# A graph layer whose lags are taken in one by one at the end, with its row fetches, register loads and feature loads regrouped

## Chip, core and metric

The kernel runs on one core of one Trainium2 chip. The time is device microseconds of one execution. Lower is better. Engines are named as in the profile: PE is TensorE (PEld its weight loads), DVE is VectorE, ACT is ScalarE, POOL is GpSimd, SP is SyncE. A queue's name with a q (SPq) means what the engine's sequencer does itself: register loads, semaphore waits, issuing of DMAs.

## The reference, cut to what matters

There are 12500 nodes with 64 features each and 200000 edges, sorted by their target node `dst`. For every edge a gate is computed from its 64 edge features and a message from the features of both end nodes; the messages are summed by target; a two-layer network on the sum is added to the node, and the result is layer-normalised.

```python
ssp = lambda x: softplus(x) - log(2)
nodes = node_state[edges].reshape(num_edges, -1)          # source and target rows, 128 wide
gates = ssp(edge_state @ We1 + be1) @ We2 + be2
gates = gates * (1 - sigmoid(5 * (edges_distance - 3.5)))
h = ssp(nodes @ Wn1 + bn1) @ Wn2 + bn2
message_sum = zeros.at[edges[:, 1]].add(h * gates)
new_state = node_state + (ssp(message_sum @ Ws1 + bs1) @ Ws2 + bs2)
out = layernorm(x + new_state)
```

## The kernel before

**Groups.** The edges are cut into 391 groups of 512, numbered g (line 62 on has the constants). As the edges are sorted by target, the 256 edges of each half of a group have targets in a window of 42 nodes, whose first node `base` is computed on the chip in a preparation stage (to about 150 us), which also builds a table of the target-side products x·Wn1+bn1.

For each group these steps exist, each a small function:

- `gather(g)` (line 166): four indirect DMAs on POOL (line 176) fetch the 512 source rows, 20 groups ahead. In a few groups, `by_rows`, only three are used: the fourth block of 128 rows comes through SP, row by row.
- `fetch(i)` (line 180): in step i SP loads ROWS = 4 row numbers into registers by one register load (line 187) and issues four one-row DMAs (line 191) into the tile `xr`. 128 rows take 32 steps, so every 32nd group is served so: 12 groups. A slot's group is transposed two steps after the step that fetches its last row.
- `load(g)` (line 195): SP fetches the group's edge features `eT` (128 KB, line 197), every second time loads four window bases into registers (line 199), and fetches two windows of 42 table rows into `wns` (line 204). It runs five groups ahead; eT and wns have seven buffers.
- `transposes` and `xcopy` (lines 217, 222): PE transposes the rows, ACT copies them out.
- `layer1_edge`, `layer1_node` (226, 228, 233): first layers into the PSUM tile `z` (two buffers).
- `exps`, `logs` (243, 246, ACT), `softplus` (251, DVE): the activation `s`.
- `layer2_edge`, `layer2_node` (257, 260, 265): second layers into `gh`.
- `hcut`, `message` (270, 274, DVE): the product of gate, cutoff and h.
- `scatter` (278, PE): one-hot matrices add the messages up by window. `window` (284, 287, DVE): each half's base goes into a register by a load of its own, then 42 columns are added to `sums`.

**Order of the work.** The order on each engine is that of the program; the scheduler is off. Step i of the main loop holds `load(i+5)`, `fetch(i)`, `gather(i+19)`, the scatter of group i-3, the second layers of group i-1, the first layers of i+1 and the transposes of i+3. So a group passes with lags of three, two and two steps. On PE a step runs: scatter, `layer2_edge`, first layers, (a node block's matmul), transposes, `layer2_node`. On DVE: softplus, window, hcut, message, one-hot. At step `both`, 12 before the last, all lags are cut at once: two groups of second layers in that step, three scatters in the next. The last group's first layer is split in two.

**Node blocks.** When all edges up to a block of 512 nodes are known to be summed (`block_steps`), the block's own network runs in five parts, one per step, between the groups: `hidden` and `clamp`; `logs` and `ssp`; `layer2` and `center`; `square` and `variance`; `root` and `store`. The block's x rows `y` are fetched by SP in `clamp` (line 312), and SP issues the store of the result in `store` (line 360), which waits for DVE's last product `y` (line 359). SP's order is that of the program, so what is behind the store waits with it. The last 512 nodes are two blocks of 256, run side by side at the end.

Of the kernel before, what the change touches and what calls it, by code (L numbers as in the profile page):

```python
# [63 lines left out]
CATCH_UP = 12  # L65
ROWS = 4
# [6 lines left out]
def node_blocks(N):  # L73

    rest = N - NB
    first = rest % NB
    assert rest > 0 and first % 2 == 0 and first <= HE
    sizes = ([first] if first else []) + [NB] * (rest // NB) + [HE, HE]
    return [(sum(sizes[:i]), n) for i, n in enumerate(sizes)]
# [12 lines left out]
def slots_by_rows(NG):  # L92

    return [g for g in range(P // ROWS + 4, NG - 2, P // ROWS)]
# [3 lines left out]
def gnn_resnorm_kernel(ctx: ExitStack, tc: tile.TileContext, a: dict, out: bass.AP, E: int):  # L98
# [52 lines left out]
    half = const.tile([P, 1], F32, name="half")  # L151
    ones3 = const.tile([PIECES, HE], BF16, name="ones3")
# [26 lines left out]

    def fetch(i):  # L180

        n, r = divmod(i * ROWS, P)
        if i < 0 or n >= len(by_rows):
            return
        if r == 0:
            xrs[by_rows[n]] = loads.tile([P, P], F32, name="xr", bufs=2)
        _, at = nc.values_load_multi_w_load_instructions(
            rows_i[n : n + 1, r : r + ROWS], engines=[SP], min_val=0, max_val=N - 1,
            skip_runtime_bounds_check_because="src holds rows of x")
        for j, v in enumerate(at):  # L190
            nc.sync.dma_start(xrs[by_rows[n]][r + j : r + j + 1, :D], x[bass.ds(v, 1), :])  # L191
# [3 lines left out]
    def load(g):  # L195
        eTs[g] = loads.tile([P, HE], F32, name="eT")
        nc.sync.dma_start(eTs[g], a["eT"][:, g, :])
        if g % 2 == 0:
            _, at = nc.values_load_multi_w_load_instructions(
                base_i[0:1, 2 * g : 2 * g + 4], engines=[SP], min_val=0, max_val=N - 1,  # L200
                skip_runtime_bounds_check_because="they were clamped to these bounds")
            bases[g], bases[g + 1] = at[:2], at[2:]
        for h in range(2):
            nc.sync.dma_start(wns[D:DW, g % REST, h, :], table[bass.ds(bases[g][h], W), :])  # L204
# [26 lines left out]
    def layer1_node(g, h):  # L231
        zn = zs[g][:, h, HE * (1 - h) : HE * (2 - h)]
        nc.tensor.matmul(zn, wns[:, g % REST, h, :], xTs[g][:, h], start=True, stop=True, skip_group_check=True)  # L233
# [29 lines left out]
    def layer2_node(g, h):  # L263
        for t in range(2):
            nc.tensor.matmul(ghs[g][:, 1, 2 * t + h, :], ss[g][:, 1 + h, t, :], wn2, start=False,  # L265
                             stop=h == 1 and t == 1, skip_group_check=True)
# [14 lines left out]

    def window(g):
        for h in range(2):
            base = nc.values_load(base_i[0:1, 2 * g + h : 2 * g + h + 1], engines=[DVE], min_val=0, max_val=N - 1,
                                  skip_runtime_bounds_check_because="it was clamped to these bounds")
            part = sums[h * D : (h + 1) * D, bass.ds(base, W)]
            nc.vector.tensor_add(part, part, scs[g][h * D : (h + 1) * D, h * W : (h + 1) * W])  # L287

    def node_block(first, n, pool):
# [20 lines left out]
        def clamp():  # L310
            t["y"] = tile3("y")
            nc.sync.dma_start(t["y"], x[rows, :].rearrange("(q p k) d -> p q k d", q=nq, k=2))
            t["l"], t["zb"] = (pool.tile([P, HE], F32, name=name, bufs=2) for name in ("l_s", "zb"))
            nc.vector.tensor_scalar(t["l"], t["z"], packed["bs1"], BIG, OP.add, OP.min)
            nc.vector.tensor_scalar(t["zb"], t["z"], packed["bs1"], None, OP.add)
# [17 lines left out]
        def center():  # L333
            nc.vector.scalar_tensor_tensor(t["y"], t["y"], 2.0, t["u"][:, :nq], OP.mult, OP.add)
            mean = small("mean")
            nc.vector.tensor_reduce(mean, t["y"], AX.X, OP.add)
            nc.vector.scalar_tensor_tensor(t["y"], mean.to_broadcast([p, nq, 2, D]), -1.0 / D, t["y"], OP.mult, OP.add)
# [5 lines left out]
        def variance():  # L343
            t["v"] = small("var")
            nc.vector.tensor_reduce(t["v"], t["y2"], AX.X, OP.add)
            nc.vector.tensor_scalar(t["v"], t["v"], 1.0 / D, EPS, OP.mult, OP.add)

        def root():
            t["r"] = small("rstd")
            nc.scalar.activation(t["r"], t["v"], AF.Ln)  # L350
            nc.scalar.activation(t["r"], t["r"], AF.Exp, scale=-0.5)

        def store():

            v, r = t["v"], t["r"]
# [4 lines left out]
            nc.sync.dma_start(out[rows, :].rearrange("(q p k) d -> p q k d", q=nq, k=2), t["y"])  # L360

        def then(f, g):
            def both():
# [4 lines left out]
        return [(hidden, clamp), (None, then(logs, ssp)), (layer2, center), (None, then(square, variance)),  # L368
                (None, then(root, store))]
# [6 lines left out]
    with tc.manual_schedule():  # L376
# [4 lines left out]
        with tc.tile_pool(name="prep", bufs=1) as prep:  # L381
# [23 lines left out]
            nc.vector.memset(half, 0.5)  # L405
            nc.vector.memset(ones3, 1.0)
# [40 lines left out]
            nc.vector.tensor_add(brow[:, 1:3, :], brow[:, 1:3, :], ps[:1, : 2 * D].rearrange("o (i d) -> o i d", d=D))  # L447
            pieces = prep.tile([1, PIECES, 4 * D], BF16, name="pieces")
# [43 lines left out]
        with tc.tile_pool(name="finish", bufs=1) as finish:  # L492
            blocks = list(zip(node_blocks(N), block_steps(N, NG)))
            last = NG - 1
            both = last - CATCH_UP
            second, third, ahead = {}, {}, {}
            for i in range(-3, NG + 1):
                groups = [i - 1] if i < both else [i - 1, i] if i == both else [i]
                second[i] = [g for g in groups if 0 <= g < NG]
                groups = [i - 3] if i <= both else [i - 3, i - 2, i - 1] if i == both + 1 else [i - 1]  # L500
                third[i] = [g for g in groups if g >= 0]
                groups = [i + 3] if i < both else [] if i == both else [i + 2]
                ahead[i] = [g for g in groups if g < NG]
            todo, complete = [], 0
# [9 lines left out]
            for i in range(-3, NG + 1):  # L514
                part = todo.pop(0) if todo else None
# [4 lines left out]
                if i < both:  # L520
                    if 0 <= i + 1:
                        zs[i + 1] = z_tile()
                    for g in third[i]:
                        scatter(g, zs[i + 1][:, 1, HE : HE + 2 * W])
                    for g in second[i]:
                        layer2_edge(g)
                elif i + 1 < last:
                    zs[i + 1] = z_tile()
                if i + 1 < last:
                    at(layer1_edge, i + 1)  # L530
                    at(layer1_node, i + 1, 0)
                    at(layer1_node, i + 1, 1)
                if part and part[0] and i + 2 < last:
                    part[0](tx_tile())
                for g in ahead[i]:
                    transposes(g)
                if i + 1 < last:
                    at(exps, i + 1)
                    if i < both:
                        at(logs, i + 1)  # L540
                for g in ahead[i]:
                    xcopy(g)
                if i >= both and i + 1 < last:
                    logs(i + 1)
                if i + 2 == last:
                    zs[last] = z_tile()
                    layer1_edge(last)
                for g in second[i]:
                    if i >= both:
                        layer2_edge(g)  # L550
                    if i + 2 == last:
                        layer1_node(last, 0)
                        layer1_node(last, 1)
                    layer2_node(g, 0)
                    layer2_node(g, 1)
                if i + 2 == last:
                    for some in (edge, node):
                        exps(last, some)
                        logs(last, some)
                if i + 1 < last:  # L560
                    at(softplus, i + 1)
                if i >= both:
                    for g in third[i][:-1]:
                        scatter(g, tx_tile()[:, : 2 * W])
                        window(g)
                    for g in third[i][-1:]:
                        scatter(g, tx_tile()[:, : 2 * W])
# [3 lines left out]
                for g in third[i][-1:]:  # L571
                    window(g)
                    complete = g + 1
                if i < both:
                    for g in second[i]:
                        hcut(g)
                        message(g)
                for g in ahead[i]:
                    at(onehot, g + 2)
                if i + 2 == last:  # L580
                    softplus(last, edge)
                    softplus(last, node)
                if part:
                    if i + 2 < last:
                        part[1]()
                    else:
                        node_part(part)
                while blocks and blocks[0][1] <= complete and i < last:
                    todo += node_block(*blocks.pop(0)[0], finish)
# [151 lines left out]
```

## Time and profile before

| | |
|---|---|
| median of 14 runs | 2598.84 us (2572.59 to 2615.81) |
| the profiled execution | 2610.76 us |
| its span, first to last instruction | 2609.0 us |
| mean granted TensorE clock | 0.828 |
| PE busy | 2237.2 us (86%) |
| POOL busy | 1468.6 us (56%), 1551 gathers of 947 ns |
| DVE, ACT busy | 1046.6 us (40%), 918.0 us (35%) |
| rows fetched by SP | 1536 DMAs of 0.2 KB |
| eT and wns | 391 DMAs of 128 KB, 782 of 21 KB |

The page counts register loads, moves, semaphore waits and the issuing of DMAs as no engine's busy time, so SP has no row in its first part; what SP does is seen in the timeline of SP, in the waits of the SP queue, and in the view of one source line. A PE that is busy for 86% need not be PE at its peak: the granted clock enters the durations.

### The profile page before, as it was taken

How to read it: one execution, taken by the hardware profiler on the slowest of the kernel's cores; microseconds unless marked ns; L12 is line 12 of the kernel's file. 1: busy time of each engine (PE TensorE's matmuls, PEld its weight loads, DVE VectorE, ACT ScalarE, POOL GpSimd, SP SyncE). 2: the span in 40 equal slices, each digit the busy share in tenths (PEclk: the TensorE clock that was granted, in tenths of full speed). 3: DMA queues.
4: the chain of work that ended last, by engine and by line, in shares of the span. 5: the costliest groups of instructions: out<-in, count | busy, mean ns of one | idle time of the engine just before them, and what ended most of it. 6: DMA issues, size and time to landing. Idle time of an engine off the chain costs nothing.

```text
span 2609.0 us, 42101 instructions
## 1 busy us (share of the span) xinstructions
PE 2237.2 (86%) x11378; PEld 1776.7 (68%) x11378; DVE 1046.6 (40%) x2752; ACT 918.0 (35%) x1322; POOL 1468.6 (56%) x1555
## 2 busy tenths in 40 slices
PE   4469888899888979898988978988999987998997
PEld 4357677677676757676777767766777765776775
DVE  4123333333444333333434443443444443444455
ACT  1133333333333323333333333333333333333443
POOL 6655666556666546655556656565566655565500
PEclk9977888677888778878879788787788877888887
DMA  7212222222222222222222222222222222222210
GB/s 196 79 46 51 50 51 53 48 49 54 50 49 52 49 50 51 54 50 52 49 53 53 51 53 48 53 51 53 53 56 51 51 50 54 55 54 55 54 47 18
DMA packets 171021, 143.15 MB, mean 55 GB/s; under 512 B 46507, under 2 KB 142947, under 8 KB 170778
## 3 DMA queue, kind: packets, MB, share of 16 engines
q1 hardware_dynamic: 119778, 87.95, 11.7%
q0 software_dynamic: 49632, 50.92, 10.8%
q10 hardware_dynamic: 1368, 1.51, 0.3%
q8 instruction: 95, 1.56, 0.3%
q14 instruction: 148, 1.21, 0.2%
HBM read 130.57 MB, written 9.63 MB: 54 GB/s over the span
## 4 chain that ended last, share of the span: by engine, by line
PE 77%; issue 9%; another core or an unknown queue 3%; DVE 3%; SPq 3%; ACT 2%; DMA 1%; POOL 1%; DVEq 0%; ACTq 0%; POOLq 0%
PE z L233 15%; PE gh L265 13%; PE z L228 10%; PE gh L260 10%; PE z L278 8%; PE tx L217 8%; PE gh L257 5%; PE z L226 3%; SPq L191 1%; PE tx L306 1%; PE z L471 1%; PE tx L330 1%; DVE h L270 1%; SPq L204 1%
## 5 line engine op out<-in xcount | busy, mean ns | idle before, releaser
L176 POOL DMA_INDIRECT xg<-in_x,src_i x1551 | 1468.4, 947 | 1002.3 <-issue 376.4
L251 DVE SCALAR_TENSOR_TENSOR s<-u,z 128x768 f32<-128x768 f32 x392 | 372.8, 951 | 1249.5 <-ACT u L246 708.8
L243 ACT ACTIVATE u<-z 128x768 f32<-128x768 f32 x392 | 317.0, 809 | 1491.2 <-PE z L233 537.1
L233 PE MATMUL z<-xT,wns 106*128 106x256 f32 x1564 | 516.6, 456 | 43.1 <-issue 37.6
L265 PE MATMUL gh<-consts,s 128*128 128x64 f32 x3128 | 456.5, 296 | 8.1 <-issue 8.1
L265 PEld LDWEIGHTS gh<-consts,s 128*128 128x128 f32 x3128 | 452.4, 222 | 4.7 <-issue 4.7
L233 PEld LDWEIGHTS z<-xT,wns 106*128 106x128 f32 x1564 | 358.5, 231 | 134.4 <-issue 64.9
L246 ACT ACTIVATE u<-u,one 128x768 f32<-128x768 f32 x392 | 365.9, 933 | 12.4
L278 PE MATMUL z<-xg,msg 128*128 128x84 f32 x1500 | 268.1, 306 | 108.0 <-DVE msg L274 43.9
L260 PE MATMUL gh<-consts,s 128*128 128x128 f32 x1564 | 326.8, 336 | 27.8 <-issue 18.9
L228 PE MATMUL z<-eT,consts 128*128 128x256 f32 x782 | 327.8, 504 | 19.8 <-issue 13.2
L260 PEld LDWEIGHTS gh<-consts,s 128*128 128x128 f32 x1564 | 240.7, 218 | 140.9 <-issue 129.6
L278 PEld LDWEIGHTS z<-xg,msg 128*128 128x128 f32 x1500 | 224.7, 215 | 121.9 <-issue 80.4
L217 PE MATMUL tx<-consts,xg 128*106 128x128 f32 x1552 | 286.8, 316 | 6.8 <-DVE xg L209 2.7
L217 PEld LDWEIGHTS tx<-consts,xg 128*106 128x106 f32 x1552 | 230.3, 156 | 72.9 <-issue 28.5
L222 ACT COPY xT<-tx 106x512 f32<-106x512 f32 x391 | 221.8, 567 | 63.4 <-PE tx L217 48.4
L270 DVE TENSOR_TENSOR h<-gh,cut 128x256 f32<-128x256 f32 x391 | 165.9, 424 | 178.0 <-PE gh L265 86.8
L228 PEld LDWEIGHTS z<-eT,consts 128*128 128x128 f32 x782 | 137.4, 218 | 79.9 <-issue 38.5
L257 PE MATMUL gh<-row,ones 3*128 3x512 bf16 x391 | 166.6, 426 | 6.6 <-issue 6.5
L274 DVE TENSOR_TENSOR msg<-gh,h 128x256 f32<-128x256 f32 x391 | 165.9, 424 | 13.5
L287 DVE TENSOR_TENSOR sums<-sums,z 64x42 f32 x750 | 144.4, 193 | 13.6 <-issue 7.2
L209 DVE TENSOR_TENSOR xg<-consts,rel 128x168 f32<-128x168 f32 x391 | 126.7, 325 | 1.1 <-issue 0.4
(79 smaller groups left out, 625.7 us busy)
## 6 DMA issues: line engine op xcount, KB each, us to landing
eT<-in_eT SPq DMA_DIRECT2D x391, 128.0 KB
xg<-in_x,src_i POOLq DMA_INDIRECT x1551
xr<-in_x SPq DMA_DIRECT2D x1536, 0.2 KB
wns<-table SPq DMA_DIRECT2D x782, 21.0 KB
table<-tb SPq DMA_DIRECT2D x14, 448.0 KB
sums<-in_xT SPq DMA_DIRECT2D x7, 455.0 KB
y<-in_x SPq DMA_DIRECT2D x23, 128.0 KB
out<-y SPq DMA_DIRECT2D x23, 128.0 KB
```

What stands on the lines that cost most here:

```text
L176: nc.gpsimd.indirect_dma_start(out=xg[:, k, :D], out_offset=None, in_=x, in_offset=bass.IndirectOffsetOnAxis(ap=src_i[:, g, k : k + 1], ax ...
L217: nc.tensor.transpose(tx[:, k, :], row, ident)
L222: nc.scalar.copy(xT, xTs[g])
L228: nc.tensor.matmul(zs[g][:, 0, :HE], we1.rearrange("a h d -> a (h d)"), eTs[g], start=False, stop=True, skip_group_check=True)
L233: nc.tensor.matmul(zn, wns[:, g % REST, h, :], xTs[g][:, h], start=True, stop=True, skip_group_check=True)
L243: nc.scalar.activation(us[g][:, part], z_of(g)[:, part], AF.Exp)
L246: nc.scalar.activation(us[g][:, part], us[g][:, part], AF.Ln, bias=one)
L251: nc.vector.scalar_tensor_tensor(ss[g].rearrange("p i t e -> p (i t e)")[:, part], us[g][:, part], BIG, z_of(g)[:, part], OP.min, OP.max)
L257: nc.tensor.matmul(gh, ones3[:, :P], row3.rearrange("q i k d -> q (i k d)"), start=True, stop=False, skip_group_check=True)
L260: nc.tensor.matmul(v[:, 0, t], ss[g][:, 0, t, :], we2, start=False, stop=False, skip_group_check=True)
L265: nc.tensor.matmul(ghs[g][:, 1, 2 * t + h, :], ss[g][:, 1 + h, t, :], wn2, start=False, stop=h == 1 and t == 1, skip_group_check=True)
L278: nc.tensor.matmul(sc, msgs[g][:, 2 * t : 2 * t + 2, :].rearrange("p h f -> p (h f)"), xgs[g][:, 2 * t : 2 * t + 2, D:DW], start=t == 0, s ...
```

## The change

Five things are changed together.

1. SP's row fetch: six rows a step instead of four, eight row numbers by one register load; slots need no longer start at a step's first row. 128 rows take 21.3 steps, which makes 17 slots instead of 12; a slot's group lies two steps later behind its last row than before.
2. SP's loads: `eT` of two groups by one DMA of 256 KB; the window bases of four groups (eight registers) by one register load.
3. DVE's `window` loads the two bases of a group by one register load.
4. Node blocks: 25 of them, the last of 512; the bias and the weights of the last layer are centred in the preparation, and x rows are fetched and centred four and two groups before the block is complete, so that after `layer2` only an addition is left; eps enters as ACT's bias; the store is a part of its own and is issued by ACT, but for the last block.
5. The order: in a step `layer2_node` now follows `layer2_edge` before the first layers. The lags are shortened one at a time, from 30 steps before the last; the last group is written out.

```diff
-CATCH_UP = 12
-ROWS = 4
+CATCH_UP = 30
+ROWS = 6
+REGS = 8
...
 def fetch(i):
-    n, r = divmod(i * ROWS, P)
...
-    _, at = nc.values_load_multi_w_load_instructions(
-        rows_i[n : n + 1, r : r + ROWS], engines=[SP], ...)
-    for j, v in enumerate(at):
-        nc.sync.dma_start(xrs[by_rows[n]][r + j : r + j + 1, :D], x[bass.ds(v, 1), :])
+    for at in range(ROWS * i, min(ROWS * (i + 1), len(by_rows) * P)):
+        n, r = divmod(at, P)
...
+        if at % REGS == 0:
+            _, row_at[:] = nc.values_load_multi_w_load_instructions(
+                rows_i[n : n + 1, r : r + REGS], engines=[SP], ...)
+        nc.sync.dma_start(xrs[by_rows[n]][r : r + 1, :D], x[bass.ds(row_at[at % REGS], 1), :])
...
 def slots_by_rows(NG):
-    return [g for g in range(P // ROWS + 4, NG - 2, P // ROWS)]
+    ends = [ceil(P * (n + 1) / ROWS) + 6 for n in range(NG)]
+    return [g for g in ends if g < NG - 2]
...
 def load(g):
-    eTs[g] = loads.tile([P, HE], F32, name="eT")
-    nc.sync.dma_start(eTs[g], a["eT"][:, g, :])
     if g % 2 == 0:
+        pair = loads.tile([P, 2, HE], F32, name="eT", bufs=LOADS // 2 + 2)
+        for j in range(min(2, NG - g)):
+            eTs[g + j] = pair[:, j, :]
+        nc.sync.dma_start(pair[:, : min(2, NG - g)], a["eT"][:, g : min(g + 2, NG), :])
+    if g % 4 == 0:
+        n = min(4, NG - g)
         _, at = nc.values_load_multi_w_load_instructions(
-            base_i[0:1, 2 * g : 2 * g + 4], engines=[SP], ...)
+            base_i[0:1, 2 * g : 2 * (g + n)], engines=[SP], ...)
...
 def window(g):
+    if g not in window_at:
+        window_bases(g)
     for h in range(2):
-        base = nc.values_load(base_i[0:1, 2 * g + h : 2 * g + h + 1], engines=[DVE], ...)
-        part = sums[h * D : (h + 1) * D, bass.ds(base, W)]
+        part = sums[h * D : (h + 1) * D, bass.ds(window_at[g][h], W)]
...
-        return [(hidden, clamp), (None, then(logs, ssp)), (layer2, center), (None, then(square, variance)),
-                (None, then(root, store))]
+        return [(None, fetch), (None, center), (hidden, clamp), (None, then(logs, ssp)), (layer2, add),
+                (None, then(square, variance)), (None, then(root, scale)), (None, store)]
...
+        def store():
+            queue = nc.sync if first + n == N else nc.scalar
...
     for i in range(-3, NG):
-        groups = [i - 1] if i < both else [i - 1, i] if i == both else [i]
+        groups = [i - 1] if i < ends + 6 else [i - 1, i] if i == ends + 6 else [i]
...
-        groups = [i - 3] if i <= both else [i - 3, i - 2, i - 1] if i == both + 1 else [i - 1]
+        groups = ([i - 3] if i < ends - 6 else [i - 3, i - 2] if i == ends - 6 else [i - 2]
+                  if i < ends + 12 else [i - 2, i - 1] if i == ends + 12 else [i - 1])
...
-        ahead[i] = [g for g in groups if g < NG]
+        ahead[i] = [i + 3] if i < ends else [i + 2] if i == ends + 1 else [i + 1] if i > ends + 2 else []
...
+    if i < ends:
...
+        for g in second[i]:
+            layer2(g)
+        if i >= -1:
+            layer1(i + 1)
```

## Prediction

> **What bounds the kernel now.** I read the page's first two parts, then the busy time by stretches, then SP's timeline, then who waits for whom. PE is the busiest engine, but the stretches show that it is not simply full. The columns below are the stretch, its length, busy time and count of the edge matmul's two passes (two per group, so half the count is the number of steps) for PE and for PEld, then clock, DMA share and GB/s.
>
> ```profile
> 160.00:2410.00 2250.00, 298.82 (x714) 125.03 (x712) 0.82 0.22 52
> 2478.00:2510.00 32.00, 4.89 (x14) 2.08 (x14) 1.00 0.16 44
> 2510.00:2565.00 55.00, 7.68 (x16) 3.19 (x16) 0.72 0.15 40
> ```
>
> In the long stretch 357 steps take 2250 us, 6.30 us each, at clock 0.82. From 2478 us on, when POOL has issued its last gather (2470.20), seven steps take 32 us, 4.57 each, at full clock. So PE can do a step in 4.6 us and has 6.3. The clock follows: where PE waits it falls, and then PE is slow for a while. Who makes PE wait? SP's timeline, first without gathers, then with them (start, time from first issue to last, line, count):
>
> ```profile
> 2481.93 0.36 SPq L197 DMA_DIRECT2D eT<-in_eT  x1
> 2482.54 0.88 SPq L204 DMA_DIRECT2D wns<-table  x2
> 2484.25 1.50 SPq L191 DMA_DIRECT2D xr<-in_x  x4
> 2485.84 0.36 SPq L197 DMA_DIRECT2D eT<-in_eT  x1
> 2486.99 0.92 SPq L204 DMA_DIRECT2D wns<-table  x2
> 2488.73 1.50 SPq L191 DMA_DIRECT2D xr<-in_x  x4
> 2490.28 0.41 SPq L312 DMA_DIRECT2D y<-in_x  x1
> 2490.79 0.41 SPq L197 DMA_DIRECT2D eT<-in_eT  x1
> ```
>
> ```profile
> 1306.92 0.70 SPq L197 DMA_DIRECT2D eT<-in_eT  x1
> 1309.06 0.53 SPq L204 DMA_DIRECT2D wns<-table  x2
> 1310.77 1.55 SPq L191 DMA_DIRECT2D xr<-in_x  x4
> 1313.79 0.01 SPq L197 DMA_DIRECT2D eT<-in_eT  x1
> ```
>
> From eT to eT SP needs 3.91 us, and 4.44 with a base load (2485.84 to 2490.79 less 0.51 for y): 4.18 on average, with no pause worth the name. With gathers running the same round takes 6.87 here, and 6.30 on average, since SP goes round once per PE step. So about 2.1 us of a round are added while POOL gathers; the trace shows that, not its cause. Is SP waiting in them? The waits of the SP queue between 160 and 2478 us (total, times, longest):
>
> ```profile
> SPq L191 <- DMA xr<-in_x: 28.7, 54, 1.2
> SPq L360 <- DVE y L359: 24.1, 5, 6.8
> SPq L197 <- PE tx L217: 8.9, 24, 0.7
> SPq L204 <- PE tx L217: 8.7, 29, 0.7
> ```
>
> All rows of that answer sum to some 105 us of 2318, none but the store's is over 1.2 us. So **SP is at work or slowed for over 95% of the main loop and is never held back by full buffers**: whatever is added to its round has nowhere to hide. And PE does wait for it, at the transposes of the row-fetched groups (busy, mean | idle before, releasers):
>
> ```profile
> L217 PE MATMUL tx<-consts,xr 128*106 128x128 f32 x12 | 4.6, 387 | 47.8 <-DMA xr<-in_x 23.8 <-DMA wns<-table 22.5 <-issue 1.5
> L278 PE MATMUL z<-xg,msg 128*128 128x84 f32 x1500 | 268.1, 306 | 108.0 <-DVE msg L274 43.9 <-issue 34.2 <-DVE h L270 22.6
> ```
>
> Twelve instructions have 47.8 us of idle before them: PE had run ahead of SP and is pulled back. The 108.0 us before the scatters are the other loop, ACT and DVE late with a message. Both are near the limit; I take SP as the one that sets the pace.
>
> **The change by its parts, per step.**
>
> *Rows.* Four rows span 1.50 us with the last issue's 0.23 (median of L191 in its source view: 228 ns), so one row is (1.50-0.23)/3 = 0.42. Two more: **+0.84**.
>
> *Register loads.* The source views give
>
> ```profile
> L187 SPq TENSOR_LOAD <-rows_i x384: 2/552/746, 151.0 to 2541.8; - x192
> L284 DVEq TENSOR_LOAD <-base_i x782: 297/303/599, 163.1 to 2594.1; - x196
> ```
>
> 303 ns for one register, 490 (L199's median) to 552 for four. Eight are not in the trace: at least 0.55, at most two loads, 1.10. I take 490-303 over three registers, 0.06 each, and so 0.80, nearest to the measured slope. Rows: 0.75 loads a step of 0.80 for one of 0.55, **+0.05** (-0.14 to +0.28). Bases: a load costs 0.53 of a round now (4.44-3.91), every second step; then 0.78 every fourth: **-0.07**.
>
> *Feature pair.* One eT issue with what precedes it is about 0.46 (0.36 and 0.10 ahead); half of them go: **-0.23**. That a transfer of 256 KB issues in the time of one of 128 KB is assumed; at twice the time the gain is zero.
>
> *Store.* 24 issues go to ACT, 0.46 each: -0.03 on SP. On ACT they come in front of the next exponential, 24 x 0.46 = 11 us in all, while ACT is busy for 35%; in a part of its own the store follows finished work.
>
> SP's own round: +0.84+0.05-0.07-0.23-0.03 = **+0.56** on 4.18. Now cover: waits that disappear once SP is the late one are the store's 24 us and the waits for PE's releases, about 50 us together in the same answer, so 75 us or 0.21 a step. Net **+0.35 a step**. Row fetching lasts 363 steps: 0.35 x 363 = +127 us. Bounds: if the slow part of a round grows with the work (6.30/4.18), 0.56 becomes 0.84, net +0.63, +229 us; if SP has cover that I don't see, 0.
>
> *Five gathers fewer* (17 slots for 12): 5 x between 0.5 (a quarter of the 2.1 us) and 2.1 us: -3 to -10, I take -7. The gathers' POOL time (5 x 0.95) lies beside PE's.
>
> *DVE's base load.* One load of 0.30 less per step, and 0.06 longer. Both loads run while the softplus does (0.95 us, L251), which hides them; where the softplus comes late up to 0.3 x 357 = 107 us of DVE's chain could go, but with SP late it is not what ends last: 0.
>
> *`layer2_node` moved.* The eight matmuls (0.84 us at full clock in the chain) now lie before the first layers. hcut's 178 us of idle on DVE shrink, z comes 0.84 us later to ACT, and the scatter's wait for the message grows by up to that. Behind it on PE stand the whole step's matmuls. Against 0.84 x the 95 waits that the scatters of the main loop have at most (80 us) stands the same sum earlier for hcut: 0, either way hidden behind SP.
>
> *Node blocks.* The same reductions and products, two steps earlier: beside other work, 0. One block fewer: one `hidden` and one layer2, 2 us of PE.
>
> *The end.* From 2510 to 2565 us eight steps take 55 us, 6.9 each, against 4.57 just before: all lags fall at once, PE waits, the clock drops. If the gradual cut avoids half of the 8 x 2.3 us: -10 (0 to -19). The tail is one block of 512, whose operations take 0.42 where the half blocks' take 0.29, but no centring stands in it: -2 (0 to -3).
>
> Sum: 127-7-2-10-2 = **+106**. The execution's own time of 2610.8 becomes 2717; it stands 12 us above the median of the 14 runs, so against the median I say **2705 us**.
>
> **A rule against this.** Six one-row DMAs have 0.2 KB each, and SP's sequencer still spends 0.42 us on every one. The Trainium skill, "DMA: Bandwidth & Descriptors", section "Issuing engines are not separate DMA queues", holds the sequencer's time to start a DMA to be usually small beside the DMA itself; by it the two rows would cost nothing, and the sum would be near 2580. Here the issue times fill SP's round, so the row decides. The same page ("Latency and other measured facts") puts a register load's floor at about 600 ns, whatever it loads; by it eight registers cost 0.60, not 0.80, and the sum is 0.20 x 0.75 + 0.05 = 0.20 a step, 72 us, lower. The single load's 303 ns on DVE contradicts the floor.
>
> **Rivals.**
>
> 1. *SP isn't the limit* (faster). For it: TensorE is 86% busy, most idle time before PE's matmuls is put to issue and messages, not to DMAs, and a slot's rows now have two steps more before they are needed. Then the 47.8 us before xr go, the end gives 12, the gathers 7, the block 2: 2611-69 = 2542, against the median 2530; if only half of the xr idle goes, 2554. Price point: net SP work of at most 0 a step. Chance 0.28, at 2520 to 2585.
> 2. *SP's added work is covered* by fewer slow spells: PE's runs at 4.6 us a step crowd POOL's gathers together, and a slower, steadier step would space them. If the slow part falls by a sixth (2.1 to 1.75), +0.35 is gone and the end's gains remain with some wait for SP: 2590 to 2610. Chance 0.10.
> 3. *The slow part grows with SP's work*: 2609+229-21, about 2805 on the median. Chance 0.10.
> 4. The forecast, SP sets the pace with +0.2 to +0.5 a step: 2640 to 2760. Chance 0.52.
>
> The bound of 0.5% is about what a measurement of this kernel can tell from no change. Faster 0.28, same 0.10, slower 0.62. For 8 in 10 the range must take in most of rival 1 and leave out rival 3's end: 2535 to 2770. The likeliest case's own range is 2640 to 2760.
>
> **What would show it.** In the changed profile: rows issued x6 in 2.3 to 2.4 us; an eT issue every second step; SP's round near 6.6 us with gathers and near 4.7 without; idle on PE before L228 and L233 put to eT and wns, and a lower clock. The register load of eight at 0.75 to 0.85. Steps from 2510 us on without a drop of the clock. I am wrong if SP's queue shows waits for PE's releases, that is, slack, and steps stay at 6.3 or fall; or if the idle before xr is gone and nothing takes its place.

## The result, and the profile after

The changed kernel takes **2874.70 us** (median of 10 runs, 2860.07 to 2888.69), before takes 2600.44 (47 runs): ratio **1.1067** [1.1038, 1.1097]. The forecast was 2705. The profiled execution spans 2899.6 us for 2609.0, at a mean clock of 0.763 for 0.828.

The kernel before itself took about 2600 us in the recorded comparison, in e5 to e8 and (2570) in e16, and about 2000 us in all other experiments, on chips 0 and 14 both, so what follows speaks of a 2600 group and a 2000 group and compares only within one; after as it stands was run in the 2600 group alone.

The changed kernel, by stretches (edge matmuls alone; length, PE, PEld, clock, DMA share, GB/s):

```profile
160.00:2410.00 2250.00, 292.14 (x649) 121.59 (x648) 0.76 0.20 47
2740.00:2790.00 50.00, 6.98 (x14) 2.89 (x14) 0.71 0.10 28
```

Where before made 357 steps in 2250 us, after makes 324: 6.93 us a step instead of 6.30. And after the last gather (2736.8 us) seven steps now take 50 us, 7.1 each, where they took 4.57. So there are two losses, one in the loop and one in the end. SP's timeline beside the gathers, for six rows a round, and the waits of SP's queue from 160 to 2740 us:

```profile
1306.17 3.37 SPq L196 DMA_DIRECT2D xr<-in_x  x6
1309.56 0.70 SPq L205 DMA_DIRECT2D eT<-in_eT  x1
1312.45 1.46 SPq L214 DMA_DIRECT2D wns<-table  x2
1316.04 3.68 SPq L196 DMA_DIRECT2D xr<-in_x  x6
```

```profile
SPq L196 <- DMA xr<-in_x: 32.0, 68, 1.3
SPq L196 <- DMA out<-y: 23.7, 1, 23.7
SPq L214 <- PE tx L227: 17.9, 61, 0.6
SPq L205 <- PE z L238: 16.6, 11, 6.1
```

Six rows take 3.4 to 3.7 us here. Where no register load falls among the six, the median in the main loop is 3.38 us, against 2.32 in e9, which has no slow instructions. SP still waits for nobody for long, the one 23.7 us apart. Then the groups that wait:

```profile
L238 PE MATMUL z<-eT,consts 128*128 128x256 f32 x782 | 354.8, 544 | 78.6 <-DMA eT<-in_eT 77.6 <-issue 0.7
L296 PE MATMUL z<-xg,msg 128*128 128x84 f32 x1432 | 267.2, 321 | 134.6 <-DVE msg L292 113.1 <-DVE h L288 12.4 <-issue 6.2
L341 DVE TENSOR_REDUCE mean<-y 128x4 f32<-128x256 f32 x24 | 10.0, 419 | 200.1 <-DMA y<-in_x 200.1
```

The first is the wait that the forecast named (features that SP brings late). The last is one that it priced at nothing: DVE's centring stands 200 us waiting for the rows `y`, and the scatters behind it wait for DVE's message (113.1 us, 43.9 before).

The same by stretches of steps, in us, from the start of the first edge matmul of each step (group 10's, 340's and so on) in the profiled executions of the 2600 group (the two executions of the unchanged kernel, after and e5, agree to 3 us in the main loop):

| | to step 10 | 10 to 340 | 340 to 360 | 360 to 390 | tail | span |
|---|---|---|---|---|---|---|
| before | 195.6 | 2088.6 | 123.6 | 172.4 | 28.7 | 2609.0 |
| e8: before, new loads, four rows | 195.6 | 2025.8 | 124.5 | 167.7 | 29.3 | 2542.9 |
| e16: before, SP's part whole | 190.4 | 2165.4 | 128.6 | 168.4 | 28.0 | 2680.8 |
| e7: after, early y, late lag | 192.6 | 2266.8 | 139.8 | 208.0 | 27.4 | 2834.5 |
| e6: after, early y | 199.4 | 2265.6 | 171.1 | 180.1 | 27.5 | 2843.7 |
| e5: after, repeated | 194.8 | 2295.9 | 179.3 | 198.2 | 22.7 | 2890.8 |
| after | 192.7 | 2298.7 | 179.0 | 201.7 | 27.6 | 2899.6 |

### The profile page after: what moved, and what is told of

It reads as the page before. It is cut to its first block, busy times and chain, and to the rows that moved or that the text cites. A ratio compares the mean times of both kernels' runs of the same rounds, so it can differ in the third digit from the quotient of the medians.

```text
span 2899.6 us, 43084 instructions
## 1 busy us (share of the span) xinstructions
PE 2411.7 (83%) x11373; PEld 1899.9 (66%) x11373; DVE 1045.6 (36%) x2750; ACT 926.9 (32%) x1317; POOL 1465.8 (51%) x1550
## 5 line engine op out<-in xcount | busy, mean ns | idle before, releaser
L245 PE MATMUL z<-xT,wns 106*128 106x256 f32 x1564 | 571.2, 496 | 79.8 <-DMA wns<-table 59.6
L279 PE MATMUL gh<-consts,s 128*128 128x64 f32 x3128 | 501.1, 309 | 61.0 <-issue 60.3
L279 PEld LDWEIGHTS gh<-consts,s 128*128 128x128 f32 x3128 | 486.5, 234 | 68.5 <-issue 68.0
L245 PEld LDWEIGHTS z<-xT,wns 106*128 106x128 f32 x1564 | 380.6, 251 | 203.7 <-issue 63.2
L238 PE MATMUL z<-eT,consts 128*128 128x256 f32 x782 | 354.8, 544 | 78.6 <-DMA eT<-in_eT 77.6
L296 PE MATMUL z<-xg,msg 128*128 128x84 f32 x1432 | 267.2, 321 | 134.6 <-DVE msg L292 113.1
L296 PEld LDWEIGHTS z<-xg,msg 128*128 128x128 f32 x1432 | 249.8, 246 | 152.1 <-issue 119.9
L273 PE MATMUL gh<-consts,s 128*128 128x128 f32 x1564 | 335.0, 346 | 11.2 <-DVE s L264 9.3
L273 PEld LDWEIGHTS gh<-consts,s 128*128 128x128 f32 x1564 | 248.4, 227 | 124.1 <-issue 111.3
L227 PE MATMUL tx<-consts,xg 128*106 128x128 f32 x1547 | 310.3, 336 | 15.8 <-issue 10.4
L227 PEld LDWEIGHTS tx<-consts,xg 128*106 128x106 f32 x1547 | 248.0, 168 | 85.1 <-issue 44.8
L238 PEld LDWEIGHTS z<-eT,consts 128*128 128x128 f32 x782 | 147.6, 236 | 143.7 <-DMA eT<-in_eT 87.5
```

The source lines that it names most:

```text
L227: nc.tensor.transpose(tx[:, k, :], row, ident)
L238: nc.tensor.matmul(zs[g][:, 0, :HE], we1.rearrange("a h d -> a (h d)"), eTs[g], start=False, stop=True, skip_group_check=True)
L273: nc.tensor.matmul(v[:, 0, t], ss[g][:, 0, t, :], we2, start=False, stop=False, skip_group_check=True)
L296: nc.tensor.matmul(sc, msgs[g][:, 2 * t : 2 * t + 2, :].rearrange("p h f -> p (h f)"), xgs[g][:, 2 * t : 2 * t + 2, D:DW], start=t == 0, s ...
```

## The experiments

Two theories went in. **S**: SP's own round is the whole loss. **O**: the new order, the node blocks and the end make it, by new waits.

**e1 to e4: one part undone or done alone (2000 group).** Edits, cut to the lines that differ:

```diff
-ROWS = 6                                  # e1, on after
+ROWS = 4
-    return [g for g in ends if g < NG - 2]    # e4, on after: one slot only
+    return [g for g in ends if g < NG - 2][:1]
-... [i - 3] if i < ends - 6 else [i - 3, i - 2] if i == ends - 6 ...   # e3, on after
+... [i - 3] if i < ends else [i - 3, i - 2] if i == ends ...
```

e2 is before with after's `fetch`, `load`, `slots_by_rows`, ROWS and REGS, and nothing else.

> The changed kernel with four rows a step instead of six, all else as changed. Theory S (SP's round sets the pace of the main loop, and its own work is stretched by about a half while POOL gathers): SP's own round falls to some 3.7 us, stretched 5.5, so SP no longer sets the pace; steps of the main loop fall from 6.9 to 6.0-6.3 us and the time to 2580-2660 us; what stays above the kernel before is the slower end. Theory O (the new order and the new waits, above all DVE waiting for the early fetch of y, set the pace): the time stays over 2800 us.

> The kernel before with only SP's part of the change: six rows a step, registers by eight, the feature pair, bases for four groups. Theory S: 2600 + 0.6 to 0.7 us for 363 steps, 2790 to 2860 us. Theory O: 2580 to 2640 us.

> The changed kernel, but the scatter's lag is cut from three to two only when the step's order changes (at 30 before the last), not six steps earlier. If the six steps between 354 and 360, which took up to 11.7 us each, are slow because their scatter waits for a message of the step just before, the time falls by 25 to 45 us to about 2840. If they are slow because SP is behind there, it stays within 15 us of 2875.

> The changed kernel with one row-fetched group instead of 17: SP fetches rows in the first 22 steps only, and POOL makes 16 gathers more. Theory S: SP's own round is then about 1.7 us, SP is never late, and the time falls to 2560-2650 us; idle of PE before the edge and table matmuls that is put to DMAs goes to under 10 us. Theory O: over 2800 us.

Measured: e1 2049.26 us, ratio 1.0274 [1.0230, 1.0318]; e2 2005.93, 1.0060 [1.0037, 1.0083]; e3 2166.79, 1.0863 [1.0832, 1.0895]; e4 2073.83, 1.0397 [1.0367, 1.0427]. The absolute numbers expected don't apply, as before takes 1994 here. The order of the four does: SP's part alone costs 0.6%, after without it 3 to 4%, both together 8.6%. ("Both together" is e3, after but for the late lag: after itself was not run in this group.) So S falls for this group, and the parts don't look additive: late SP and the new order together cost more than the sum. In e3 DVE waits 150.4 us for y (20 times), in e1 7.0 us, in e4 not at all. But e2, with the old node blocks, has 101.6 us of the same wait and loses only 0.6%.

**e5 to e8 (2600 group).** Edits: e5 none; e6 and e7

```diff
-if blocks and complete >= blocks[0][1] - 4 and not centered:   # y's fetch
+if blocks and complete >= blocks[0][1] - 9 and not centered:
```

with e3's edit also in e7; e8 is e2 with ROWS = 4.

> The kernel of after, unchanged, for its ratio to before beside the other runs of this call. If the cost is mainly the lateness of SP, the ratio falls where before itself is fast (steps near 4.4 us leave SP's round of six rows less covered, but the sequencers take fewer long instructions): 1.03 to 1.06 there. If it is the order and its new waits (the centring on DVE behind a late fetch of y, the cut of the lag), it stays at 1.08 to 1.11 wherever it runs.

> After, with the rows y of a node block fetched nine groups before the block is whole instead of four. If the centring that waits for y makes the long pairs of steps (12 and 7 us at each of the 24 node blocks, where two steps take 9 to 10), those 24 pairs lose 5 to 8 us each: 100 to 190 us less than after unchanged on the same chip. If SP's own round is the limit, the wait on DVE goes but the time stays within 20 us of after's, since SP's instructions are the same in number.

> The same, and scatters keep their lag of three groups until the order of the last thirty steps begins, instead of six steps before it. If the message just before its scatter makes the six steps of 11.5 us, a further 20 to 45 us less than with y early alone; within 15 us of it otherwise.

> Before, with the new loads on SP (eight rows' registers by one load, bases by four groups, features by pairs) but still four rows a step and the slots that go with them. If SP's round sets the pace as forecast, 0.25 to 0.35 us less in each of some 360 steps: 60 to 125 us less than before where before takes 2600, ratio 0.95 to 0.98. If PE or POOL sets the pace on this chip, within 1% of before.

Measured (two runs each): e5 2894.42, 1.1080 [1.0924, 1.1236]; e6 2836.52, 1.0859 [1.0686, 1.1031]; e7 2840.44, 1.0874 [1.0717, 1.1030]; e8 **2550.06, 0.9762 [0.9617, 0.9907]**.

The early y takes 58 us off (47 in the span: 30 in the main loop, 26 in the last fifty steps, less some at the start): neither the 100 to 190 of O nor the "within 20" of S. The groups of e6 show why the 200 us of DVE's wait gave back so little:

```profile
L238 PE MATMUL z<-eT,consts 128*128 128x256 f32 x782 | 347.7, 534 | 145.8 <-DMA eT<-in_eT 130.1 <-issue 13.6 <-DMA wns<-table 1.8
L296 PE MATMUL z<-xg,msg 128*128 128x84 f32 x1432 | 262.4, 317 | 56.3 <-DVE msg L292 36.4 <-DVE h L288 13.1 <-issue 3.8
```

The message's wait falls by 77 us, and 53 come back one matmul later as a wait for eT: behind the late y there was SP. The late cut of the lag moves the loss (31 us less in steps 340 to 360, 28 more in 360 to 390) and saves nothing, so that expectation of 20 to 45 us missed. e8 fell 54 us against the 60 to 125 expected, with a ratio inside the 0.95 to 0.98 named. e5 repeats the result; what the ratio is where before is fast, its other question, stays open.

Not all of the 26 us at the end is y's. 15 of them lie between the first edge matmuls of groups 373 and 379: 49.4 us at a clock of 0.62 in e5, 34.0 at 0.95 in e6, and 49.3 at 0.62 again in e7, which has the early y too. DVE waits for no y there in any of the three. What set the clock in that stretch no run shows.

**e9 to e12 and e13 to e15 (2000 group).** e9, e13 are e2 again, e10 is e1 again. e12, e14: after with ROWS = 4, the edits of e6 and e3 and CATCH_UP = 16 for 30. e11 and e15 are before without the gather of each group's third block, so a quarter of the source rows is left out:

```diff
-            if padding(g, k):
+            if k == 2 or padding(g, k):
                 nc.vector.memset(xg[:, k, :D], 0.0)
```

> SP's part of the change alone in the order of before, for a chip on which before takes about 2600. As forecast (0.35 us a step for 361 steps): 2700 to 2740. If the part of SP's round that is stretched beside the gathers grows with it (0.63 a step): 2800 to 2840. If the new order, blocks and end make nearly all of the loss: under 2640.

> After with four rows a step, for a chip on which before takes about 2600 and before with the new loads and four rows takes 2550. The two rows and their slots gone, what is left above 2550 is the new order, the node blocks and the end: 2600 to 2640 by the waits seen (58 us for the late y, 20 to 40 for the end). Near 2550 if those cost nothing of their own and only showed SP's lateness; over 2700 if they are the main loss.

> Before, with the third block of every group set to zero on DVE instead of gathered (a quarter of the source rows is left out). If SP's instructions are stretched by the gathers, as the 2.1 us of slow instructions in each round suggest, a quarter of it goes, 0.5 us a step: 2400 to 2450. If the long instructions have another cause and SP's number of instructions alone sets the pace: 2570 to 2610. Where POOL sets the pace, less too, but then SP waits for PE for most of the time.

> After with four rows a step, y fetched nine groups before its block, the lag of three kept up to the new order of the end, and that end begun 16 groups before the last instead of 30. If rows, late y and the end hold the whole loss, it is within 15 us of before with the new loads and four rows (2550 where before is 2600). If the move of layer 2, the eight parts of a node block or the output's store cost something by themselves, 2580 or more.

> SP's part alone in the order of before, where before takes about 2600. As forecast (0.35 us a step): 2700 to 2740. If the stretched part of SP's round grows with it (0.63): 2800 to 2840. If the order, blocks and end are nearly all of the loss: under 2640. Where before takes 2000: 2000 to 2010, as before.

> After with four rows, early y, late cut of the lag and an end of 16 groups, where before takes about 2600: within 15 us of 2550 if rows, late y and the end are the whole loss; 2580 or more if the move of layer 2, the eight parts or the store by ACT cost something too.

> Before without the gather of the third block (a quarter of the source rows left out, set to zero on DVE), where before takes about 2600: 2400 to 2450 if the gathers stretch SP's instructions, with about three quarters of the slow instructions of before in the trace; 2570 to 2610 and as many slow instructions if they have another cause.

Measured: e9 1.0036 [1.0011, 1.0062], e13 1.0015 [0.9981, 1.0049]; e10 1.0275 [1.0235, 1.0315]; e12 0.9997 [0.9968, 1.0027], e14 1.0013 [0.9973, 1.0052]; e11 0.9402 [0.9366, 0.9437], e15 0.9384 [0.9296, 0.9473]. Before took about 2000 in all, so the numbers expected for 2600 stay unanswered; the one given for 2000, in e13, came true. What follows for this group: from e10 to e12 the end falls from 318.9 to 269.1 us (steps 340 to 390; 248.8 in e9), the main loop stays (1594.4, 1592.6). So the end that begins 30 steps early costs some 70 us with four rows too; begun 16 steps early with a late cut of the lag, 20. And the two rows cost nothing, because here POOL sets the pace: the stretches of e10 (four gathers a group) and e15 (three), then of e9 (six rows):

```profile
160.00:1700.00 1540.00, 228.24 (x636) 96.69 (x636) 0.98 0.26 66
```

```profile
160.00:1600.00 1440.00, 223.68 (x640) 95.15 (x640) 1.00 0.25 65
```

```profile
160.00:1700.00 1540.00, 228.76 (x632) 96.82 (x632) 0.96 0.26 66
```

4.84, 4.50 and 4.87 us a step. A gather starts every 1.25 us, and a group has 3.95 of them: 4.9 us. Six rows bring SP's round, undisturbed, to just that length.

**e16 (2600 group): SP's part alone again.**

> As before, for a chip on which before takes about 2600. SP's part alone: 2700 to 2740 as forecast; 2800 to 2840 if the stretched part of SP's round grows with the two rows; under 2640 if order, blocks and end make nearly all of the loss. The main loop of after with early y (2266 us for 330 steps, against 2026 with the new loads and four rows) speaks for 2780 to 2820.

Measured (two runs): 2687.62 us, **1.0486 [1.0341, 1.0631]**, 87 us above the recorded median of before and 118 above that of its own group (three runs, 2556 to 2600). The time lies below the 2700 to 2740 expected; the ratio, put on a before of 2600, gives 2727. So it is nearest to the forecast's own step, not to the grown one, and "2780 to 2820" missed. Its main loop:

```profile
160.00:2410.00 2250.00, 296.41 (x690) 123.32 (x690) 0.80 0.19 50
```

345 steps, 6.52 us each: +0.22 a step on before's 6.30.

**e17, e18 (2000 group): the rest.** e17 is e6 with `layer2_node` behind the transposes as in before; e18 adds e3's edit and CATCH_UP = 16, still with six rows.

```diff
                     for g in second[i]:
-                        layer2(g)
+                        layer2_edge(g)
...
                     for g in ahead[i]:
                         xcopy(g)
+                    for g in second[i]:
+                        layer2_node(g)
```

> After with y fetched nine groups ahead, and the matmuls of layer 2 for the nodes put back behind the transposes, as in before; nothing else. On the chip where before takes 2600, the 330 steps of the main loop took 2266 us with the early y alone, twice, and 2165 in before with SP's part. If the new place of these matmuls is the rest of the loss (some 55 pauses of 0.7 us inside them, against 2 in their old place, and the lower clock behind each), the loop falls by 50 to 100 us, to 2165 to 2215, and the ratio to before from 1.086 to about 1.05 to 1.065. If the pauses are only where SP's lateness shows, the loop stays within 15 us of 2266 and other lines pause instead. Where before takes 2000 no such pauses are expected: 2010 to 2080.

> After with six rows, but y early, the lag of three kept up to the end's order, that order begun 16 groups before the last, and layer 2 for the nodes behind the transposes again. What is left of the change is SP's part, the eight parts of a node block, the cut weights and the store by ACT. Where before takes 2600: if the place of the matmuls is the rest of the loop's loss, the 330 steps of the main loop fall from 2266 us (early y alone) to 2165 to 2215, steps 340 to 390 from 348 to about 300, and the ratio is 1.045 to 1.065, near SP's part alone (1.049). If not, the loop stays within 15 us of 2266 and the ratio is 1.07 or more. Where before takes 2000: within 1.5% of before, as SP's part alone was, since the six long steps and the late y are gone.

Measured: e17 2062.68 and 2106.78 us; e18 2031.50, 1.0159 [1.0087, 1.0232]. Both met the 2000 group, and no pauses inside L279 are seen there with either place of the matmuls, so the question put to them is not answered. The 2000 us forecasts fit in part: e17's two runs lie inside and above 2010 to 2080, and e18's 1.6% is just over the 1.5% named. Two other things can be read. With six rows the main loop takes 1722.8 us in e3, 1624.1 in e17 (its longer run) and 1607.9 in e18. The 150.4 us that DVE waits for y in e3 are gone in both; but both also have `layer2_node` back in its old place, so that the early y alone gives this is likely and not shown (with four rows, e10, the new place costs the loop nothing: 1594.4). And what e18 keeps of the change (eight parts a block, the cut weights, the store by ACT) costs nothing in the loop: e2 has 1611.8.

## Why the prediction was wrong

It had the sign and the first mechanism, and missed by 170 us. Of the signs it named, the idle before the first layers put to eT and wns (77.6 and 59.6 us in after), the lower clock and the price of the eight-register load came; an end without a drop of the clock did not (0.71 from 2740 us on). By its steps:

**SP sets the pace, +0.35 a step, +127: right in kind; +0.23 a step in the profiled execution, +87 to +118 us in the medians (e16).** The price of SP's own work was good. This is SP's round per step in the main loop, split by its instructions' starts (slow: 0.64 to 0.76 us to the next one, register loads left out; waits: over 0.76 at a semaphore, or over 1.5). The split is rough: a slow instruction's own work counts as slow, and "the rest" holds 0.7 to 0.8 us a step of instructions of 1.0 to 1.5 us in the 2600 group:

| us a step | slow | waits | the rest | step |
|---|---|---|---|---|
| before | 1.95 | 0.17 | 4.21 | 6.33 |
| e8 | 2.24 | 0.27 | 3.63 | 6.14 |
| e16 | 1.70 | 0.05 | 4.81 | 6.56 |
| e6 | 2.23 | 0.10 | 4.54 | 6.87 |
| after | 2.13 | 0.18 | 4.65 | 6.97 |
| e9 (2000 group) | 0.02 | 0.00 | 4.85 | 4.87 |

From before to e16 the rest, which holds SP's own work, grew by 0.60 (forecast 0.56), the waits gave 0.12 (forecast 0.21), and the slow part, which the forecast held constant, fell by 0.25: net +0.23, +77 us for 330 steps. That is what rival 2 described; it took back part of the price, not all. In e8 the rest fell by 0.58 and the slow part rose by 0.29. So "whatever is added has nowhere to hide" was too strong, and rival 3, whose 2805 is the nearest number, came nearest by chance: with SP's part alone the slow part shrank instead of growing. The eight-register load took 777 ns (median of L193 in after) for the 800 assumed. The Trainium skill, "DMA: Bandwidth & Descriptors", section "Latency and other measured facts", gives a floor of about 600 ns for a register load; eight registers lie above it here, and DVE's load of one, at 303 ns in before, lies below it.

**Node blocks, "two steps earlier: beside other work, 0": wrong, and 58 us come back when y is asked for earlier (e5 to e6).** SP's order decides when y is asked for, and the centring stands two steps behind that place, on DVE in front of the next softplus. In after, up to step 349, SP issues y's fetch 3 or 4 steps behind its place in the program (its place, and the step whose first edge matmul PE had begun: 167 and 171, 185 and 189, 216 and 220, 256 and 260). A SP that is late by more than two steps turns the early centring into a wait, at 19 of the 25 blocks and of up to 13.9 us. In e10, with four rows, SP is 3 steps ahead to 2 behind, and that wait is 4.4 us in all.

The move of the blocks did not make this wait. Before, too, asks for y (in `clamp`) two steps ahead of its use (in `center`), and e16, which has before's blocks and six rows, waits almost as long. The first operation on y in before, and the same in e16:

```profile
L334 DVE SCALAR_TENSOR_TENSOR y<-y,tx 128x256 f32<-128x256 f32 x23 | 9.6, 416 | 11.1 <-DMA y<-in_x 11.0
```

```profile
L344 DVE SCALAR_TENSOR_TENSOR y<-y,tx 128x256 f32<-128x256 f32 x23 | 9.7, 421 | 166.9 <-DMA y<-in_x 166.9
```

Up to step 362 SP is mostly 1 to 3 steps late in before and 2 to 4 in e16, whose scatters wait 83.5 us for DVE's message (43.9 in before). So e16's loss may hold some of this wait already; before's order with six rows and an early y was not run. The prediction made SP late, named the waits for eT and wns, and left the due time of SP's third customer, y, as it was: that is the step that failed.

**The end, -10 and -2: wrong, some +55 us.** The stretch from step 340 to 390 takes 380.7 us for 296.0, and e16 has before's 297.0. 26 of the 85 go in e6, 15 of them by the clock stretch named above; 54 are left against e16, the end's own. Cutting the scatters' lag to two while the old order of the step still holds makes a serial loop: the scatter at the step's head needs the message that DVE made at the end of the step before. PE and DVE of after (start, busy, count, idle before):

```profile
2601.54 1.12 PE L296 MATMUL z<-xg,msg 128*128 128x84 f32 x4 [5.90 <-DVE msg L292]
...
2612.88 1.06 PE L227 MATMUL tx<-consts,xg 128*106 128x128 f32 x4
2619.36 1.15 PE L296 MATMUL z<-xg,msg 128*128 128x84 f32 x4 [5.42 <-DVE msg L292]
```

```profile
2616.35 0.95 DVE L264 SCALAR_TENSOR_TENSOR s<-u,z 128x768 f32<-128x768 f32 x1 [12.39 <-ACT u L259]
...
2618.88 0.42 DVE L292 TENSOR_TENSOR msg<-gh,h 128x256 f32<-128x256 f32 x1
```

PE's last work of a step ends near 2613.9, DVE's message at 2619.3, and only then the next step begins; four such steps of 11.5 to 11.7 us follow one another, at a clock of 0.54. With the late cut (e7) the same four steps take 29.0 us for 46.8 in e6, so the serial loop makes them long; but the whole end of e7 (347.8 us for 351.2) is hardly shorter, 15 us of the clock stretch being against it, so this loop alone does not account for the 54. In the 2000 group an end begun 16 steps before the last, with the late cut, gave 50 of 70 us back (e10 to e12). The prediction saw steps of 6.9 us where before cuts all lags at once and expected a gradual cut to be cheaper; spread over more steps, it was dearer in both groups.

**`layer2_node` moved, 0: open.** Main loops of e6 and e16 differ by 100 us that no run has explained. They come from two sets of runs whose before differ by 34 us (2604 and 2570), so up to a third of the 100 may be that, by this estimate. In the table above e6 has 0.53 us more of slow instructions a step than e16, though SP does the same work but for the stores. Its gathers bunch more: bursts of eight (pauses over 2 us part the bursts) come 54 times in the main loop of e6, 57 in after, 47 in before and 38 in e16, and a burst of eight holds more slow instructions than two of four (see the last section). Another mark is on PE: idle time inside the group of the moved matmuls,

```profile
L279 PE MATMUL gh<-consts,s 128*128 128x64 f32 x3128 | 501.1, 309 | 61.0 <-issue 60.3
```

against, at their old place in e16,

```profile
L275 PE MATMUL gh<-consts,s 128*128 128x64 f32 x3128 | 469.5, 302 | 6.7 <-issue 6.7
```

Inside the groups of eight, starts lie over 0.6 us apart 82 times in after, 54 in e6, 3 in e16: PE's own issue is slow there while short matmuls run. Whether their place makes the loss or only shows it was to be told by e17 and e18, which met the other group. The parts of node blocks and the store by ACT are in the difference as well; they cost nothing in e18's group.

**Sum, in spans, from run to run:** 72 us from before to e16 (SP's part), 47 from e6 to e5 (y asked for late, with the 15 of the clock), 54 and 100 from e16 to e6 (the end, and the unexplained part of the loop), and the remaining 18 are start, tail and the 9 between the two executions of after. The forecast had +106 for all. So the terms put at 0 or below, node blocks, end and order, hold about two thirds of the loss, and for the largest of them the cause stays open.

## What to carry to other kernels

When a change makes a queue later, list everything that this queue fetches and compare each due time with the new lateness: here y was asked for two steps ahead of its use, and SP became 3 or 4 steps late. Undo one part and do one part alone: here 0.6% (e2) and 2.7% (e1) stood beside 8.6% for nearly the whole change (e3). Of the change, the grouped loads alone look worth keeping: with four rows and the old order (e8) they beat before by 2.4% (0.9 to 3.8%, two runs) where it takes 2600 us; in the 2000 group that kernel was not run.

## What the runs showed of the hardware

**Slow issue near gathers, in one group of runs only.** In the 2600 group, instructions of SP in the second half of each burst of indirect gathers follow one another at some 0.7 us, whatever they do. The register operations ahead of the row DMAs, in before and in e9 (min/median/max ns):

```profile
L191 SPq FUSED_REGOPS  x1536: 2/37/1161, 151.6 to 2544.1; - x192
```

```profile
L196 SPq FUSED_REGOPS  x2176: 37/37/42, 84.4 to 1853.0; - x198
```

In its main loop before has 2.4 us of it per burst of four gathers and about 7 per burst of eight (instructions of 0.64 to 0.76 and of 1.0 to 1.5 us counted), e9 none with the same gathers of 0.95 us. So gathers are where it shows, but not enough to cause it; what else differs between the groups is not known. The preparation differs too: step 10 is reached after 190 to 200 us in the 2600 group and 117 to 126 in the other. In the 2000 group fewer gathers gave 6%, but by POOL's pace, so e11 and e15 say nothing on the slow issue.

**The clock halves after short pauses, and for long.** In before's main loop the clock was halved 59 times, for 764 us together, median 13.7 us each; the longest pause of PE in the 6.8 us ahead of a drop was 1.2 us in the median. Of 38 pauses of 1.2 us or more that began at full clock, 32 were followed by a drop within 6.8 us. After had 75 drops and 1106 us. e15, whose PE has one pause over 0.15 us in that loop, kept the full clock throughout. The Trainium skill, "TensorE: Matmul & The Clock Gate", section "What's actually happening", lets the clock fall after an idle window of about 3.4 us; here pauses of a third of that came before the drop, so the measurement decides.

**A store on another queue can hold SP.** In e10 SP waits 323.5 us, 19 times, up to 25.8, before a row fetch for the store that ACT issues; the two queues' DMAs use the same semaphores in turn (eight in e10's trace), and each waits for the one that used its semaphore before. No cost of it shows there (e10's main loop is 17 us shorter than e2's), since SP had slack; in after, whose SP is late, it shows once (23.7 us).
